# A sparse graph-attention kernel: the self edge as a copied tile, row lists over all columns, two gathered extra tiles instead of three

## The chip, the cores and the metric

The kernel runs on one core of a Trainium2 chip. A core has a matrix engine (TensorE; PE in the profile, its weight loads PEld), a vector engine (VectorE, DVE), an activation engine (ScalarE, ACT), GpSimd (POOL), a sync engine that issues transfers (SyncE, SP), and 16 DMA engines that all of its queues share. The metric is the time of the whole program on the device in microseconds; lower is better.

## What is computed

Two layers over a graph of 3327 nodes with 128 features. The adjacency matrix is dense in storage and sparse in content: about 65 of 3327 entries of a row are not zero, and the diagonal always belongs to them (the self edge).

```python
h = relu(layernorm(x))
for each of 4 heads:
    x1, x2 = h @ w1, h @ w2
    E = leaky_relu(x1[:, None, :] + x2[None, :, :], 0.01)
    s = exp(8 * tanh((E @ a) / 8)) * adj          # scores count only where adj is not zero
    out = leaky_relu((s / s.sum(-1, keepdims=True)) @ h @ Wlin.T, 0.01)
x = x + concatenate(outs) @ w
h = relu(layernorm(x))
A = adj + eye;  D = A.sum(1) ** -0.5
x = x + relu((D[:, None] * A * D[None, :]) @ (h @ W.T + b))
```

The costly part is the first layer's score of every edge: 128 sums, a ReLU and a weighted sum for each of 4 heads. The kernel works them out for edges only.

## The kernel before

The nodes are padded to 3328 and cut into 26 row blocks of 128, and each row block into two half blocks of 64 rows (HALF). There are 52 half blocks, worked through in order. A table in HBM has a row of 709 floats (COLS) for every node: 64 columns with the adjacency weights of the current half block's rows, the node's features h, score parts, and its 512 products x2. There are two such tables, one for even and one for odd half blocks; `weights` (L573) rewrites the 64 weight columns of one while the other is in use. Row 3328 of the table is all zeros.

**The lists (`prep`, one generator for each row block).** For each of its 128 rows the kernel lists the columns that are not zero. `code` holds 3328 minus the column number, so that zero means "no edge". Line 402 multiplies (adj is not zero) with `code`, in four parts of 832 columns. Line 406 takes the eight largest codes of each of 64 segments of 52 columns (MAX8). From these, `cand` keeps, for each half of the columns, 136 candidates: four for each of 32 segments and the eight largest of the rest. Lines 435 and 437 then take the 32 largest (SLOTS) of each half of the columns, by four rounds of MAX8 and MATCH_REPLACE8 over that half's 136 candidates: 64 slots for a row. Lines 458 and 461 take up to 40 more (EXTRA) by rounds over both halves together, 272 candidates. The slots become the row numbers of the gathers: `idx` (L451). The extras of all rows of a half block are packed one behind another into three tiles of 128 places (OVT): `lower` and a matrix product (L479) give each row its first place, `oi` (L496, L498) is the 0/1 matrix of 128 rows by 768 places that says which row owns which place, and `idxo` (L521) holds the table rows for these places. If a list or the tiles don't suffice, `flag` is raised, and the program ends with a dense computation of both layers, which this data doesn't need.

**The gathers (`gather`).** A half block has four windows of 8 tiles `g`, each of 128 table rows, and one more window `ge` with its OVT extra tiles. Line 563 issues one indirect transfer for each tile from POOL: 4 x 8 + 3 = 35 for each half block, 1820 in all. There are four buffers for `g` windows and one for `ge`.

**The scores.** A window of 8 tiles is worked in two groups m, and the extra tiles are group 8. `stage_z` transposes the 512 products of each tile with PE into the PSUM tile `z` (L588); there are two of these. For groups 0 to 7 DVE takes the maximum with the rows' own term, which gives `r` (L600); for group 8 the own term is added by a matrix product with `oi` (L591) and ACT applies the ReLU (L597). `stage_r` (L611) sums over features with PE, `finish` makes the exponentials and the weighted sums (L619 to L659; L666 to L677 for the extra tiles), `close` the block's end and the first half of layer 2.

**The order.** The program order is written out by hand. A counter `slot` runs through the groups, six slots to a group; in each slot `advance` moves the `prep` of the next row block on by its share of 72 steps (each `yield` is one), `fetch` issues the gathers whose buffer has come free, and the small steps of `finish` and `close` get their turn. So DVE's instructions for the next block's lists stand between the `r` operations of this block, on one engine that works in order. PE also turns the next block's adjacency rows (L356); ACT copies them into `at` (L358, a ring of four buffers, `pat`) and stores them (L361).

SP issues the adjacency loads (L343), the tables' weight columns (L573), `hTb` (L425), `xn_d` (L727) and a few more. Its instructions wait in order like those of any engine.

Of the kernel before, what the change touches and what calls it, by code (L numbers as in the profile page):

```python
# [9 lines left out]
F32 = mybir.dt.float32  # L10
AF = mybir.ActivationFunctionType
OP = mybir.AluOpType
AX = mybir.AxisListType
PSUM = bass.MemoryType.PSUM

P = 128
# [45 lines left out]
HALF = 64  # L62
OVT = 3
ROW = 720
COLS = 709
# [164 lines left out]
def _sparse_layers(tc, nc, x, adj, w1, w2, a, wlin, w, gw, gb, gb_sb, gwT, x_sb, dinv, flag, ident, out):  # L230
# [24 lines left out]
    with ExitStack() as l0:  # L255
# [25 lines left out]
        pb = l0.enter_context(tc.tile_pool(name="pb", bufs=2))  # L281
        pat = l0.enter_context(tc.tile_pool(name="pat", bufs=4))
        ph = l0.enter_context(tc.tile_pool(name="ph", bufs=2))
# [18 lines left out]
        nc.vector.tensor_scalar(hoff[:, :1], rowid, float(HALF), float(OVT * P), op0=OP.is_ge, op1=OP.mult)  # L302
        nc.vector.tensor_scalar(hoff[:, 1:], hoff[:, :1], float(OVT * P), None, op0=OP.add)
        nc.vector.tensor_scalar(rowid, hoff[:, :1], -HALF / (OVT * P), rowid, op0=OP.mult, op1=OP.add)
# [40 lines left out]
        def prep(b, k):  # L345

            adjb = blks[b].adjb
            csum = pb.tile([P, 4], F32, name="csum")
            deg = pb.tile([P, 1], F32, name="deg")
# [47 lines left out]
            for sgm in range(64):  # L397
                if sgm % 32 == 0:
                    codes = pa.tile([P, 2, part], mybir.dt.uint16, name="codes")
                    for i in range(2):  # L400
                        c0 = (sgm // 16 + i) * part
                        nc.vector.scalar_tensor_tensor(codes[:, i], adjb[:, c0:c0 + part], 0.0, code[:, c0:c0 + part],  # L402
                                                       op0=OP.not_equal, op1=OP.mult, accum_out=csum[:, sgm // 16 + i:sgm // 16 + i + 1])
                        yield
                c = sgm // 32
# [25 lines left out]
            k.lists = lists  # L431
            for c in range(2):
                for r in range(SLOTS // 8):
                    top = lists[:, SLOTS * c + 8 * r:SLOTS * c + 8 * r + 8]
                    nc.vector.max(top, cand[:, c, :SOME])
                    yield
                    nc.vector.match_replace(out=cand[:, c, :SOME], in_to_replace=top, in_values=cand[:, c, :SOME], imm_value=0.0)
                    yield

# [14 lines left out]
            yield  # L454
            flat = cand[:, :, :SOME]
            for r in range(EXTRA // 8):
                top = lists[:, 64 + 8 * r:64 + 8 * r + 8]
                nc.vector.max(top, flat)
                yield
                if r < EXTRA // 8 - 1:  # L460
                    nc.vector.match_replace(out=flat, in_to_replace=top, in_values=flat, imm_value=0.0)
                yield

# [24 lines left out]
            miss = pb.tile([P, 1], F32, name="miss")  # L488
            nc.vector.tensor_reduce(miss, csum, AX.X, OP.add)
            nc.vector.tensor_tensor(miss, lsum, miss, OP.not_equal)  # L490
# [4 lines left out]
            oi = pb.tile([P, 2 * OVT * P], F32, name="oi")  # L495
            nc.vector.tensor_scalar(oi, code[:, :2 * OVT * P], ext[:, 40:41], None, op0=OP.is_le)  # L496
            yield
            nc.vector.scalar_tensor_tensor(oi, code[:, :2 * OVT * P], end, oi, op0=OP.is_gt, op1=OP.mult)  # L498
            k.oi = oi
# [52 lines left out]
        def gather(b, hb, w):  # L552
# [3 lines left out]
            if w == NW:  # L556
                g, n, at = pe_.tile([P, OVT, WIDE], F32, name="ge"), OVT, k.idxo[:, hb]
            else:
                g, n, at = rows_in(), WT, k.idx[:, w, WT * hb:WT * hb + WT]
# [748 lines left out]
```

## Time and profile before

| | us |
|---|---|
| median of 3 runs | 3226.23 (3220.43 to 3227.33) |
| profiled execution, first to last instruction (span) | 2534.6 |
| median less that span | 691.6 |
| PE busy | 2282.7 (90%) |
| DVE busy | 2030.0 (80%) |
| POOL busy | 1792.0 (71%) |
| ACT busy | 705.3 (28%) |
| 16 DMA engines, share of the span by queue | POOL 71.1%, SP 19.1%, ACT 6.9% |
| moved | 838.58 MB |

The span is counted from the first to the last instruction that the profiler shows; the time of a run is that of the whole program, and the profiled execution has no separate one. A line of the profile's groups gives line, engine, operation, the tile that is written and those read, the count, then the busy time in us, the mean in ns of one, and how long the engine was idle just before, with what ended most of that idle time. A line of a timeline gives start and duration in us. Names are those of the code, without buffer numbers: `g`, `ge`, `z`, `r`, `lists`, `cand`, `oi`.

### The profile page before, as it was taken

Reading aid. Unit: us, or ns where it says so; the run is one execution under the profiler, and the core shown is the slowest. Engines: PE = TensorE matmul, PEld = TensorE weight load, DVE = VectorE, ACT = ScalarE, POOL = GpSimd, SP = SyncE. Lnnn points to the kernel's source line nnn. Section 1 sums busy time; section 2 is a strip of 40 time slices with the busy share of each in tenths; the row PEclk is TensorE's granted clock in tenths of the full one; section 3 lists DMA queues with packets and bytes.
Section 4 is the critical chain, followed back from the end, with each engine's and each line's share of the span. In section 5 each row is a group of like instructions: output and inputs, shape, how many; then the busy total and the mean of one; then the engine's idle time right before and its main releaser. Section 6 shows DMA issues by size and latency. Waiting matters only on the chain.

```text
span 2534.6 us, 51985 instructions
## 1 busy us (share of the span) xinstructions
PE 2282.7 (90%) x19410; PEld 1590.3 (63%) x19410; DVE 2030.0 (80%) x6260; ACT 705.3 (28%) x1651; POOL 1792.0 (71%) x1873
## 2 busy tenths in 40 slices
PE   6689999989988998999999999999999899999898
PEld 3466666666666666666666666666666666675553
DVE  7588988788887888888889888987988888795443
ACT  4122233223223222322322332232232223222110
POOL 3577777777777777777777777777777777777620
PEclk9699999999999999999999999999999999999999
DMA  9999999999999999999999999999999999999995
GB/s 298 389 333 334 332 357 317 329 352 334 315 338 343 319 327 358 324 328 344 339 316 340 355 314 338 348 334 321 343 344 317 324 361 314 332 323 343 328 333 196
DMA packets 460758, 838.58 MB, mean 331 GB/s; under 512 B 209098, under 2 KB 318164, under 8 KB 457172
## 3 DMA queue, kind: packets, MB, share of 16 engines
q0 software_dynamic: 145600, 640.34, 71.1%
q1 hardware_dynamic: 219396, 140.96, 19.1%
q10 hardware_dynamic: 95504, 53.88, 6.9%
q8 instruction: 156, 2.56, 0.4%
q14 instruction: 102, 0.84, 0.1%
HBM read 765.93 MB, written 113.42 MB: 347 GB/s over the span
## 4 chain that ended last, share of the span: by engine, by line
PE 36%; DVE 22%; DMA 20%; POOL 12%; issue 8%; ACT 0%; SPq 0%; DVEq 0%; POOLq 0%; ACTq 0%
DMA g<-table,idx 12%; POOL g L563 11%; DVE r L600 10%; PE z L588 10%; PE s L611 6%; DMA ge<-table,idxo 3%; PE z L591 3%; DMA AT_d<-at 2%; PE z L938 2%; DVE cand L406 2%; PE tr L628 2%; PE ag L659 2%; PE tr L371 1%; POOL ge L563 1%; DVE codes L402 1%
## 5 line engine op out<-in xcount | busy, mean ns | idle before, releaser
L563 POOL DMA_INDIRECT g<-table,idx x1664 | 1613.9, 970 | 568.4 <-issue 450.7
L588 PE MATMUL z<-ident,g 128*128 128x128 f32 x6656 | 929.9, 279 | 143.5 <-DVE r L600 106.2
L600 DVE TENSOR_TENSOR r<-z,x1n 128x1024 f32<-128x1024 f32 x832 | 1009.4, 1215 | 55.8 <-PE z L588 54.0
L588 PEld LDWEIGHTS z<-ident,g 128*128 128x128 f32 x6656 | 748.7, 142 | 361.7 <-DVE r L600 219.6
L611 PE MATMUL s<-r,sel 128*32 128x512 f32 (+1 forms) x3744 | 491.8, 598 | 0.7 <-ACT ssb L619 0.7
L619 ACT COPY ssb<-s 128x512 f32<-128x512 f32 x260 | 147.0, 565 | 533.9 <-PE s L611 531.4
L631 DVE TENSOR_TENSOR sc<-tr,g 128x32 f32<-128x32 f32 x208 | 38.4, 185 | 303.4 <-PE tr L628 303.4
L406 DVE MAX8 cand<-codes 128x8 f32<-128x52 uint16 x1664 | 214.9, 203 | 0.0
L563 POOL DMA_INDIRECT ge<-table,idxo x156 | 155.2, 995 | 49.0 <-issue 33.5
L639 ACT ACTIVATE th<-sc 128x32 f32<-128x32 f32 x260 | 58.3, 224 | 418.4 <-DVE sc L634 417.7
L591 PE MATMUL z<-oi,x1b 128*128 128x384 f32 x416 | 172.2, 496 | 0.0
L659 PEld LDWEIGHTS ag<-g,wt 128*32 128x32 f32 x3328 | 99.4, 110 | 115.4 <-issue 101.7
L358 ACT COPY at<-tr 128x512 f32<-128x512 f32 (+1 forms) x175 | 97.2, 555 | 215.9 <-PE tr L356 206.3
L628 PE MATMUL tr<-ident,ssb 128*128 128x128 f32 x988 | 152.6, 275 | 3.0 <-ACT at L358 2.7
L611 PEld LDWEIGHTS s<-r,sel 128*32 128x32 f32 x3744 | 73.9, 108 | 110.8 <-issue 86.6
L588 PEld LDWEIGHTS z<-ident,ge 128*128 128x128 f32 x624 | 80.7, 145 | 97.0 <-issue 27.7
L597 ACT ACTIVATE r<-z 128x768 f32<-128x768 f32 x104 | 84.4, 811 | 200.4 <-PE z L591 200.4
L659 PE MATMUL ag<-g,wt 128*32 128x133 f32 x3328 | 134.0, 279 | 0.0
L588 PE MATMUL z<-ident,ge 128*128 128x128 f32 x624 | 111.5, 282 | 23.3 <-DMA ge<-table,idxo 20.0
L356 PE MATMUL tr<-ident,adjb 128*128 128x128 f32 x676 | 107.8, 282 | 22.6 <-DMA adjb<-in_adj_dram 13.5
L628 PEld LDWEIGHTS tr<-ident,ssb 128*128 128x128 f32 x988 | 114.8, 141 | 11.1 <-ACT ssb L619 7.9
L402 DVE SCALAR_TENSOR_TENSOR codes<-adjb,code 128x832 uint16<-128x832 f32 x104 | 102.2, 1019 | 12.6 <-DMA adjb<-in_adj_dram 12.6
(188 smaller groups left out, 2347.4 us busy)
## 6 DMA issues: line engine op xcount, KB each, us to landing
adjb<-in_adj_dram SPq DMA_DIRECT2D x26, 1664.0 KB, 9.8
table<-AT_d SPq DMA_DIRECT2D x52, 832.0 KB, 17.0
AT_d<-at ACTq DMA_DIRECT2D x150, 256.0 KB, 5.7
g<-table,idx POOLq DMA_INDIRECT x1664
table<-img SPq DMA_DIRECT2D x12, 1312.0 KB, 4.9
adjb<-AT_d SPq DMA_DIRECT2D x18, 512.0 KB
g<-AT_d SPq DMA_DIRECT2D x7, 1024.0 KB
g<-AT_d ACTq DMA_DIRECT2D x5, 1024.0 KB, 11.0
```

What stands on the lines that cost most here:

```text
L356: nc.tensor.transpose(pt[:, q, :], adjb[:, (j0 + q) * P:(j0 + q + 1) * P], ident)
L358: nc.scalar.copy(at[:, :n, :], pt[:, :n, :])
L402: nc.vector.scalar_tensor_tensor(codes[:, i], adjb[:, c0:c0 + part], 0.0, code[:, c0:c0 + part], op0=OP.not_equal, op1=OP.mult, accum_out= ...
L406: nc.vector.max(cand[:, c, 8:].rearrange("p (r s) -> p r s", s=32)[:, :, sgm % 32], codes.rearrange("p a b -> p (a b)")[:, sgm % 32 * SEG: ...
L563: return nc.gpsimd.indirect_dma_start(out=g[:, t, lo:COLS], out_offset=None, in_=tab, in_offset=bass.IndirectOffsetOnAxis(ap=at[:, t:t + 1 ...
L588: nc.tensor.matmul(z[:, i, q * P:(q + 1) * P], g[:, m % 2 * 4 + q, PROJ + h * D:PROJ + (h + 1) * D], ident, is_transpose=True, start=(q == ...
L591: nc.tensor.matmul(z[:, i, :n], k.x1b[:, h * D:(h + 1) * D], k.oi[:, hb * n:(hb + 1) * n], start=False, stop=True, skip_group_check=True)
L600: nc.vector.tensor_tensor(r.rearrange("p h (i s) -> p h i s", s=16), z.rearrange("p h (i s) -> p h i s", s=16), k.x1n[:, 2 * hp:2 * hp + 2 ...
L611: nc.tensor.matmul(k.s[32 * h:32 * h + 32, :n], sel[:, h, 31 - at:63 - at], rs[h // 2][:, h % 2, :n], start=(at == 0), stop=(at == 1 or m ...
L619: nc.scalar.copy(ssb[:, :nk * P], s[:, :nk * P])
L628: nc.tensor.transpose(pt[:, q, :], ssb[:, q * P:(q + 1) * P], ident)
L659: nc.tensor.matmul(ag[32 * cg:32 * cg + 32, u, :WORK], wt[:, t].rearrange("p h q -> p (h q)"), g[:, t, FEAT:FEAT + WORK], start=(w == 0 an ...
```

## The change

- The self edge is taken out of the row's codes before the lists are made: in the part of the columns that holds the block's own 128, one scalar_tensor_tensor makes the negated diagonal and its sum, and an add takes it out. In two of the 26 blocks the own columns cross from one part into the next, and both parts do this.
- The 64 slots are the 64 largest codes of the whole row: eight rounds over 272 candidates, in place of four rounds over 136 for each half of the columns. The 40 extras follow by five more such rounds, as before.
- The extra tiles of a half block are still three, but only two (FOUND) are gathered. The third holds the half block's own 64 table rows, which SP copies from the table in one plain transfer; its other 64 rows are set to zero once. `oi` keeps its shape; DVE fills the two found tiles' part, and ACT copies the identity into the third's.
- The tile `ge` is allocated once and kept; the ring `pat` has three buffers instead of four.

```diff
+FOUND = 2
-        pat = l0.enter_context(tc.tile_pool(name="pat", bufs=4))
+        pat = l0.enter_context(tc.tile_pool(name="pat", bufs=3))
 ...
-        nc.vector.tensor_scalar(hoff[:, 1:], hoff[:, :1], float(OVT * P), None, op0=OP.add)
+        nc.vector.tensor_scalar(hoff[:, 1:], hoff[:, :1], float(FOUND * P), None, op0=OP.add)
 ...
                         nc.vector.scalar_tensor_tensor(codes[:, i], adjb[:, c0:c0 + part], 0.0, code[:, c0:c0 + part],
                                                        op0=OP.not_equal, op1=OP.mult, accum_out=csum[...])
+                        lo, hi = max(c0, b * P), min(c0 + part, (b + 1) * P)
+                        if lo < hi:
+                            diag = pb.tile([P, P], F32, name="lq", bufs=1)[:, :hi - lo]
+                            mine = codes[:, i, lo - c0:hi - c0]
+                            nc.vector.scalar_tensor_tensor(diag, mine, -1.0, ident[:, lo - b * P:hi - b * P], op0=OP.mult, op1=OP.mult,
+                                                           accum_out=csum[:, sums[0]:sums[0] + 1])
+                            nc.vector.tensor_tensor(mine, mine, diag, OP.add)
+                            sums[0] += 1
 ...
-            for c in range(2):
-                for r in range(SLOTS // 8):
-                    top = lists[:, SLOTS * c + 8 * r:SLOTS * c + 8 * r + 8]
-                    nc.vector.max(top, cand[:, c, :SOME])
-                    yield
-                    nc.vector.match_replace(out=cand[:, c, :SOME], in_to_replace=top, in_values=cand[:, c, :SOME], imm_value=0.0)
-                    yield
+            flat = cand[:, :, :SOME]
+            def select(r):
+                top = lists[:, 8 * r:8 * r + 8]
+                nc.vector.max(top, flat)
+                yield
+                if 8 * r + 8 < 2 * SLOTS + EXTRA:
+                    nc.vector.match_replace(out=flat, in_to_replace=top, in_values=flat, imm_value=0.0)
+                yield
+            for r in range(SLOTS // 4):
+                yield from select(r)
 ...
+            for r in range(SLOTS // 4, SLOTS // 4 + EXTRA // 8):
+                yield from select(r)
 ...
             oi = pb.tile([P, 2 * OVT * P], F32, name="oi")
-            nc.vector.tensor_scalar(oi, code[:, :2 * OVT * P], ext[:, 40:41], None, op0=OP.is_le)
-            yield
-            nc.vector.scalar_tensor_tensor(oi, code[:, :2 * OVT * P], end, oi, op0=OP.is_gt, op1=OP.mult)
+            places = [t.rearrange("p (c e) -> p c e", c=2)[:, :, :FOUND * P] for t in (oi, code[:, :2 * OVT * P])]
+            own = oi.rearrange("p (c u e) -> p c u e", c=2, e=HALF)[:, :, 2 * FOUND:]
+            for u in range(2):
+                nc.scalar.activation(own[:, :, u], ident.rearrange("p (c e) -> p c e", c=2), AF.Copy, scale=1.0 - u)
+            nc.vector.tensor_scalar(places[0], places[1], ext[:, 40:41], None, op0=OP.is_le)
+            yield
+            nc.vector.scalar_tensor_tensor(places[0], places[1], end, places[0], op0=OP.is_gt, op1=OP.mult)
 ...
             if w == NW:
-                g, n, at = pe_.tile([P, OVT, WIDE], F32, name="ge"), OVT, k.idxo[:, hb]
+                if b + hb == 0:
+                    state["over"] = pe_.tile([P, OVT, WIDE], F32, name="ge")
+                    nc.vector.memset(state["over"][HALF:, FOUND:], 0.0)
+                g, n, at = state["over"], FOUND, k.idxo[:, hb]
+                rows = b * P + HALF * hb
+                nc.sync.dma_start(g[:HALF, FOUND, :COLS], tables[hb][rows:rows + HALF, :COLS])
```

More of the change, by code (lines that the diff above doesn't have):

```diff
@@ L347, in prep @@
             adjb = blks[b].adjb
-            csum = pb.tile([P, 4], F32, name="csum")
+            csum = pb.tile([P, 6], F32, name="csum")
+            sums = [4]
             deg = pb.tile([P, 1], F32, name="deg")
@@ L454, in prep @@
             yield
[L455 to L458, printed above, removed]
-                yield
-                if r < EXTRA // 8 - 1:
-                    nc.vector.match_replace(out=flat, in_to_replace=top, in_values=flat, imm_value=0.0)
-                yield
+            for r in range(SLOTS // 4, SLOTS // 4 + EXTRA // 8):
+                yield from select(r)
             dv = pb.tile([P, 3], F32, name="dv", bufs=4)
@@ L488, in prep @@
             miss = pb.tile([P, 1], F32, name="miss")
-            nc.vector.tensor_reduce(miss, csum, AX.X, OP.add)
+            nc.vector.tensor_reduce(miss, csum[:, :sums[0]], AX.X, OP.add)
             nc.vector.tensor_tensor(miss, lsum, miss, OP.not_equal)
```

## The prediction

> **What bounds the kernel now.** I read the page's head first, then the wait list, then the timelines of one row block.
>
> ```profile
> span 2534.6 us, 51985 instructions
> PE 2282.7 (90%) x19410; PEld 1590.3 (63%) x19410; DVE 2030.0 (80%) x6260; ACT 705.3 (28%) x1651; POOL 1792.0 (71%) x1873
> ...
> L563 POOL DMA_INDIRECT g<-table,idx x1664 | 1613.9, 970 | 568.4 <-issue 450.7
> ...
> L563 POOL DMA_INDIRECT ge<-table,idxo x156 | 155.2, 995 | 49.0 <-issue 33.5
> ```
> POOL looks 71% busy, but nearly all its idle time is "issue": 0.30 us ahead of every gather, released by nothing. Its timeline:
>
> ```profile
> 1249.86 0.94 POOL L563 DMA_INDIRECT ge<-table,idxo  x1 [0.30 <-DMA AT_d<-at]
> 1251.11 0.95 POOL L563 DMA_INDIRECT ge<-table,idxo  x1 [0.30 <-issue]
> 1252.36 0.95 POOL L563 DMA_INDIRECT ge<-table,idxo  x1 [0.30 <-issue]
> 1253.61 1.19 POOL L563 DMA_INDIRECT g<-table,idx  x1 [0.30 <-issue]
> ```
> One gather starts every 1.25 us from 103 to 2381 us, with hardly a pause: 35 x 1.25 plus the longer ones is a half block's 44.9 us. POOL sets the pace. How much would PE and DVE win if it were faster? The wait list says (PE and PEld see the same stalls twice):
>
> ```profile
> DVE sc L631 <- PE tr L628: 306.2, 105, 7.6
> ...
> PEld z L588 <- DMA g<-table,idx: 33.6, 50, 2.1
> ...
> PEld z L588 <- DMA ge<-table,idxo: 24.9, 26, 2.3
> ...
> PE z L588 <- DMA g<-table,idx: 21.8, 33, 1.8
> ...
> PE z L588 <- DMA ge<-table,idxo: 20.0, 24, 2.0
> ```
> Only 25 to 58 us of 2534.6: PE meets the gathers about once in a block, at the extra tiles of its second half. So a second bound lies close behind POOL. The end of one block's DVE work shows it, DVE first, then PE:
>
> ```profile
> 1259.57 0.29 DVE L435 MAX8 lists<-cand 128x8 f32<-128x136 f32 x1
> ...
> 1260.17 1.21 DVE L600 TENSOR_TENSOR r<-z,x1n 128x1024 f32<-128x1024 f32 x1
> ...
> 1263.63 0.28 DVE L437 MATCH_REPLACE8 cand<-lists,cand 128x136 f32<-128x136 f32 x1
> 1270.23 0.19 DVE L631 TENSOR_TENSOR sc<-tr,g 128x32 f32<-128x32 f32 x1 [6.32 <-PE tr L628]
> ```
> ```profile
> 1259.70 0.33 PE L588 MATMUL z<-ident,ge 128*128 128x128 f32 x1
> 1260.98 0.33 PE L588 MATMUL z<-ident,ge 128*128 128x128 f32 x1 [0.94 <-DMA ge<-table,idxo]
> 1262.14 0.33 PE L588 MATMUL z<-ident,ge 128*128 128x128 f32 x1 [0.84 <-DMA ge<-table,idxo]
> ```
> From 1222.8 to 1263.9 DVE never stops: codes, MAX8 and list rounds lie between its r operations, and PE's next z waits for r ("z L588 <- DVE r L600" 107.2 us). PE begins the extra tiles at 1259.70, right behind the r that ends at 1259.65, waits 1.8 us for the gathers, and then works 8 us alone while DVE idles 6.3. A block is two such DVE stretches (about 40 and 38 us) and two PE stretches.
>
> **Gathers.** 52 of 1820 go. POOL's path gets 52 x (0.995 + 0.30) = 67 us shorter, 2.6 us per block. That is time only as far as PE waited for gathers. I take the stall at the extra tiles, 25 us (24 steady blocks x 1.04), since it lies where DVE is idle anyway; the g stalls lie in the start-up block (seven of them, 6.7 us, in PE's timeline from 76 to 122 us) and inside continuous DVE work, and I take none of them. Ends: 20 us (the PE row of ge alone) and 58 us (both PEld rows). Term: -25.
>
> **List rounds.** Eight rounds of MAX8 and MATCH_REPLACE8 now run over 272 candidates instead of 136. The rows for both sizes:
>
> ```profile
> L435 DVE MAX8 lists<-cand 128x8 f32<-128x136 f32 x208 | 61.4, 295 | 1.3
> L437 DVE MATCH_REPLACE8 cand<-lists,cand 128x136 f32<-128x136 f32 x208 | 59.0, 284 | 0.0
> L458 DVE MAX8 lists<-cand 128x8 f32<-128x272 f32 x130 | 57.3, 441 | 2.7
> ...
> L461 DVE MATCH_REPLACE8 cand<-lists,cand 128x272 f32<-128x272 f32 x104 | 44.3, 426 | 0.0
> ```
> (441-295) + (426-284) = 288 ns a round, 2.30 us a block, 60 us in all. The counts and the places in DVE's order stay. In the block above four rounds and the fifth's MAX8 stand ahead of the r (1260.17) after which PE owns the time: 4 x 0.288 + 0.146 = 1.30 us, in a stretch without DVE idle time. The rest falls into the 6.3 us idle behind it. 24 x 1.30 = +31. Ends: 0 (all absorbed) and 24 x 2.30 = 55.
>
> **Self edges.** Each block gets one scalar_tensor_tensor over 128 with an accumulator (nearest: L725, the same form, 0.279 + a read of 0.08) and one add (nearest: L377, 0.273), each waiting for the one before: 0.60 us, twice in the two blocks whose own columns cross a part's border. They stand inside the 40 us DVE stretch, so on the path: 24 x 0.60 = +14 (ends 0 and 17).
>
> **The selection matrix oi.** 512 columns instead of 768 on DVE: a third of 0.53 and of 0.94 (L496 and L498, from start to next start) is 0.18 + 0.31, of which start-up doesn't shrink; I take 0.42, in DVE's other stretch, where PE waits for L498 by name. 24 x 0.42 = -10 (ends 0 and -12). The two ACT copies cost about 0.2 each (nearest: L474, 0.194) on an engine that is 28% busy: 0, and if their cover went, +10.
>
> **Own rows.** One SP transfer of 64 rows per half block, about 0.47 us to issue (the table store L573 took that). It waits for PE's L677 and DVE's am of the half block before; there L677 ended at 1239.6. Behind it on SP stand hTb (went at 1237.5, would slip 2 us, and is first read by L527, some 65 us later), the adjb load (1250.7), the weights' store (1262.4) and xn_d: none is reached sooner than 1239.6 but hTb. So 0; a table store that slipped by those 2 us would add 2 us to 52 half blocks at most, 104, but its 17 us to landing end long before POOL needs it. PE transposes as many tiles as before; its third z of the extra tiles now waits for this transfer, sent some 10 us ahead of the two gathers. The memset of the unused half runs once, beside a DVE wait of 1.99 us at 34 us: 0.
>
> **Ring of "at".** A block's seven copies stand 3.2 us apart (1226.5 to 1246.0), so with three buffers one comes free after 9.7 us against a landing of 6.7 median, 14.0 at most. A few ACT waits of up to 4 us, behind ACT's idle time: 0, with +10 as the far end.
>
> **First block.** Its DVE work is 2.9 us later, but the first gather (66.5) came 6.8 us after its indices (59.7), and PE then waits for gathers (79.9) and adjb (86.1): 0. The last block has no list work behind it and layer 1 is untouched: 0.
>
> **Sum.** -25 + 31 + 14 - 10 = +10 us on the span of 2534.6. The profiled execution has no time of its own beside its span; the runs' median, 3226.23, stands 691.6 above it, which I carry over. 3226.2 + 10 = 3236, 0.3% slower.
>
> A rule from the Trainium skill speaks against the transfer's move: "DMA: Bandwidth & Descriptors", section "Issuing engines are not separate DMA queues", says that DMAs from all engines run on the same 16 DMA engines, so that another issuer saves only issue time. The trace agrees that these are nearly full (busy share 0.99 from 300 to 2300 us), yet POOL's even step shows that issue time is what counts. If the shared engines were the bound, only the bytes of 64 rows would be saved: a gather took 71.1% x 2534.6 / 1820 = 0.99 us of them, half of it by 52 is 26 us, not 67. The sum above stays below either.
>
> **Rivals.** A, faster: the DVE stretch has slack and POOL's relief comes through. For it: POOL's unbroken step. Against it: 41 us with no DVE gap. Price: all PE-row stalls go (20 + 21.8 = 42), oi gives 10, the self edges cost 14: 3188. It decides where DVE's added time ahead of the last r stays below 25/24 = 1.04 us a block. B, no change: gain and additions cancel, 3226; for this the terms need be off by only 4 us. C, slower still: a new wait takes the old one's place, as the 6.3 us of DVE idle shrink and all eight rounds reach the path: 24 x (2.30 + 0.60) - 25 - 10 + 10 for the ring = +45, 3271. D, the change doesn't hold on this data and the dense fallback runs, at a price that no row here shows: counted from the inputs, the fullest half block needs 240 of its 256 extra places, so 1 in 100.
>
> **How the numbers follow.** Chances: forecast 0.42, A 0.23, B 0.21, C 0.13, D 0.01. What separates from no change here is 0.2%, 6.4 us. Slower 0.42 + 0.13 + 0.01 = 0.56, same 0.21, faster 0.23. The range: down to 3203, which leaves about half of A below; up to 3262, half of C above. The forecast's own is 3233 to 3250. All lower ends together (-58 + 0 + 0 - 12 = -70) would give 3156, all upper ones (-20 + 55 + 17 + 0 + 20 = +72) 3298; that they fall together is in what is left out.
>
> **What would show it.** In the profile after: POOL's gathers stop at PE's L659 and its steps are no longer even (if they are even and the span is 40 us or more shorter, A). "z <- DMA ge" is gone from PE's waits. MAX8 and MATCH_REPLACE8 in the list lines take 441 and 426 throughout; DVE busy is near 2030 + 60 + 16 - 12 = 2094. The wait "z <- DVE r" is longer than 107. I am wrong if DVE shows gaps between the list rounds, or SP's own-rows transfer holds a table store.

## The result: 3% slower, outside the range, and a second level of times

| | us | ratio to before (95%) |
|---|---|---|
| before, median of 4 | 3223.33 (3216.62 to 3227.33) | |
| changed, median of 4 | 3321.82 (3316.31 to 3326.16) | 1.0297 [1.0265, 1.0329] |

The forecast was 3236, with a range of 3203 to 3262: the sign was right, the size was not, and 3322 lies above the range. (One run of e12 below, 4481, and one of e16, 3894, stand far above the others of their kernels, and no figure here includes them.)

The page of the changed kernel, its head, its chain and the two list rows:

```profile
span 3314.4 us, 52238 instructions
PE 2614.3 (79%) x19410; PEld 1787.3 (54%) x19410; DVE 2116.4 (64%) x6345; ACT 702.4 (21%) x1703; POOL 1734.2 (52%) x1821
...
PEclk8789988899999888998999899888899899999999
...
PE 50%; DVE 17%; another core or an unknown queue 16%; ACT 6%; issue 5%; DMA 3%; POOL 1%; ACTq 0%; SPq 0%; DVEq 0%; POOLq 0%
...
L446 DVE MAX8 lists<-cand 128x8 f32<-128x272 f32 x338 | 148.3, 439 | 4.1
...
L449 DVE MATCH_REPLACE8 cand<-lists,cand 128x272 f32<-128x272 f32 x312 | 132.8, 426 | 0.0
```

And its waits (who waited for what, us in total, times, longest):

```profile
POOL g L581 <- PE ag L677: 741.5, 172, 11.0
DVE sc L649 <- PE tr L646: 418.3, 112, 8.4
...
DVE r L618 <- remote: 227.8, 87, 12.2
...
PE z L606 <- DVE r L618: 222.5, 129, 7.5
...
ACT ssb L637 <- remote: 202.3, 27, 15.2
...
PE z L606 <- DMA g<-table,idx: 4.5, 6, 1.5
```

The shown profile of before has a span of 2534.6 us, and nothing in the change can add 780 us. This run of the changed kernel took 3316.31, so only 1.9 us lie outside its span of 3314.4; nothing like the 691.6 us that I carried over is there. POOL, which hardly paused in the shown profile of before, now waits 741.5 us for PE to free its buffers. And a releaser appears that the shown profile of before does not have: "remote", or in the chain "another core or an unknown queue", which stands here, on one core, for a wait whose end the trace can't put down to an instruction that had just finished.

**Two levels.** The runs that follow were made in groups; each group ran on one chip, with runs of the kernel before among them. All runs of a group share one of two levels: before took 2532, 2532 and 2533 in three groups and 3301, 3300 and 3224 in three others, beside the 3223 of the table above. One chip had both, in different groups. The timed runs of before and of the change stand at the upper level; the profile that I read stands at the lower one. No run of before at 3223 has a profile; e7, at 3280, stands in for them below. So there are two questions: what the change does at each level, and why.

### The profile page after: what moved, and what is told of

It reads as the page before. It is cut to its first block, busy times and chain, and to the rows that moved or that the text cites. A ratio compares the mean times of both kernels' runs of the same rounds, so it can differ in the third digit from the quotient of the medians.

```text
span 3314.4 us, 52238 instructions
## 1 busy us (share of the span) xinstructions
PE 2614.3 (79%) x19410; PEld 1787.3 (54%) x19410; DVE 2116.4 (64%) x6345; ACT 702.4 (21%) x1703; POOL 1734.2 (52%) x1821
## 4 chain that ended last, share of the span: by engine, by line
PE 50%; DVE 17%; another core or an unknown queue 16%; ACT 6%; issue 5%; DMA 3%; POOL 1%; ACTq 0%; SPq 0%; DVEq 0%; POOLq 0%
PE z L606 17%; PE s L629 10%; DVE r L618 8%; PE z L609 4%; PE tr L646 4%; ACT r L615 2%; PE tr L373 2%; PE tr L358 2%; PE ag L677 2%; DVE cand L416 2%; ACT ssb L637 2%; PE z L956 2%; ACT adjb L437 1%; DMA g<-table,idx 1%
## 5 line engine op out<-in xcount | busy, mean ns | idle before, releaser
L581 POOL DMA_INDIRECT g<-table,idx x1664 | 1612.1, 969 | 1337.9 <-PE ag L677 741.5
L606 PE MATMUL z<-ident,g 128*128 128x128 f32 x6656 | 1051.4, 303 | 324.7 <-DVE r L618 222.5
L606 PEld LDWEIGHTS z<-ident,g 128*128 128x128 f32 x6656 | 857.2, 157 | 566.0 <-DVE r L618 331.6
L629 PE MATMUL s<-r,sel 128*32 128x512 f32 (+1 forms) x3744 | 569.1, 619 | 24.0 <-issue 18.8
L646 PE MATMUL tr<-ident,ssb 128*128 128x128 f32 x988 | 176.8, 305 | 121.8 <-ACT ssb L637 87.0
L677 PE MATMUL ag<-g,wt 128*32 128x133 f32 x3328 | 194.1, 282 | 77.6 <-issue 76.0
L677 PEld LDWEIGHTS ag<-g,wt 128*32 128x32 f32 x3328 | 119.6, 111 | 223.2 <-issue 205.2
L581 POOL DMA_INDIRECT ge<-table,idxo x104 | 98.7, 949 | 107.2 <-PE ag L695 52.0
L373 PE MATMUL tr<-at,x_sb 128*128 128x128 f32 x488 | 82.9, 316 | 89.9 <-ACT at L360 61.2
L446 DVE MAX8 lists<-cand 128x8 f32<-128x272 f32 x338 | 148.3, 439 | 4.1
L449 DVE MATCH_REPLACE8 cand<-lists,cand 128x272 f32<-128x272 f32 x312 | 132.8, 426 | 0.0
```

The source lines that it names most:

```text
L373: nc.tensor.matmul(pq[:, :P], x_sb[:, j0 + q, :], at[:, q, :], start=(q == 0), stop=(q == js[-1]))
L581: return nc.gpsimd.indirect_dma_start(out=g[:, t, lo:COLS], out_offset=None, in_=tab, in_offset=bass.IndirectOffsetOnAxis(ap=at[:, t:t + 1 ...
L606: nc.tensor.matmul(z[:, i, q * P:(q + 1) * P], g[:, m % 2 * 4 + q, PROJ + h * D:PROJ + (h + 1) * D], ident, is_transpose=True, start=(q == ...
L629: nc.tensor.matmul(k.s[32 * h:32 * h + 32, :n], sel[:, h, 31 - at:63 - at], rs[h // 2][:, h % 2, :n], start=(at == 0), stop=(at == 1 or m ...
L646: nc.tensor.transpose(pt[:, q, :], ssb[:, q * P:(q + 1) * P], ident)
L677: nc.tensor.matmul(ag[32 * cg:32 * cg + 32, u, :WORK], wt[:, t].rearrange("p h q -> p (h q)"), g[:, t, FEAT:FEAT + WORK], start=(w == 0 an ...
```

## Experiments

### The kernel before, profiled again (e0, e7)

No edit.

> The kernel before, unchanged, profiled again. What is asked: the shown profile of before had a span of 2534.6 us where its runs took 3226; the profile after has a span of 3314.4 for a run of 3316.3, 2 us outside it. Theory 1 (the shown profile of before was no picture of its timed runs: in those, PE, DVE and ACT pace it, not POOL): span about 3221, 2 us below the time; a half block about 57 us instead of 44.9; POOL's gathers wait for PE's L659 in hundreds of us as they do after. Theory 2 (the 691.6 us are a fixed part outside the span, and the change itself cost them): span again near 2535, POOL's gathers 1.25 us apart.

> The kernel before, unchanged, once more with a profile beside these runs. At the lower level: span near 2531, POOL's gathers 1.25 us apart. At the upper level: span near 3221, and its waits show what holds the kernel there before any change: by theory 1, ACT and DVE waiting for landings of transfers, and POOL waiting for PE.

At the lower level (e0) a run of 2532.97 us, at the upper (e7) one of 3279.99. The page of e0 and some of its waits, then the page of e7:

```profile
span 2531.0 us, 51985 instructions
...
PE 34%; DVE 26%; DMA 19%; POOL 12%; issue 8%; ACT 0%; SPq 0%; DVEq 0%; POOLq 0%; ACTq 0%
```
```profile
PE z L588 <- DVE r L600: 110.8, 152, 2.0
...
PE z L588 <- DMA ge<-table,idxo: 22.5, 25, 2.3
...
POOL g L563 <- PE ag L659: 7.2, 4, 2.2
```
```profile
span 3278.1 us, 51985 instructions
PE 2595.6 (79%) x19410; PEld 1764.9 (54%) x19410; DVE 2049.7 (63%) x6260; ACT 688.1 (21%) x1651; POOL 1798.1 (55%) x1873
...
PE 44%; DVE 19%; another core or an unknown queue 16%; issue 7%; DMA 6%; ACT 5%; POOL 2%; SPq 0%; ACTq 0%; DVEq 0%; POOLq 0%
```

The waits of e7:

```profile
POOL g L563 <- PE ag L659: 579.7, 178, 10.3
DVE sc L631 <- PE tr L628: 455.5, 107, 8.8
...
DVE r L600 <- remote: 276.4, 100, 5.7
...
PE z L588 <- DVE r L600: 170.2, 161, 6.8
```

Theory 1 of the expectations holds: in both, 1.9 us or so lie outside the span, and at the upper level the kernel before already shows POOL waiting for PE and the "remote" waits. The 691.6 us were the distance of the two levels. At the upper level POOL waits 580 us for PE before anything is changed, so less work on POOL has no wait of PE to shorten there.

What sits behind "remote" can be read from the semaphore records of the trace. PE's records give its matmuls an end that is modelled. In e0, 1 of PE's 2416 recorded semaphore updates comes over 1 us after the end of the instruction that makes it; in e7 574 of 2243 do, by up to 7.3 us, while DVE's and ACT's come within 0.02 us in both, but for a handful. So at the upper level PE's results are later than its rows say. The traces of the upper level also hold only about half as many semaphore updates as those of the lower (e7 22512, e0 43969; of DVE's, 2451 and 3873), so who ended a wait is less certain there, and part of "remote" may be records that are missing. In e7 the weight loads of L659 also come 0.68 to 0.75 us apart in over 90 places, in e0 in none. And PE's granted clock is 0.5 in 104 stretches (516 us together) against 17 (96 us). The Trainium skill, "TensorE: Matmul & The Clock Gate", Part 1, says that PE's clock is at half after an idle window of about 3.4 us and at full again after a busy one of about that length. The stretches fit the second (66 of the 104 last 3.4 us, the only shares are 0.5 and 1); whether each follows an idle window can't be read, since PE's rows end too early there. As an estimate, half speed costs at most half of the 420 us that came on top, 210 of the 747 us between the two spans: it can't be the whole difference. What makes PE late at the upper level is not shown by any run here.

### The whole change and its ring at the lower level (e8, e1, e2)

e8 has no edit against the changed kernel. e1:
```diff
-        pat = l0.enter_context(tc.tile_pool(name="pat", bufs=3))
+        pat = l0.enter_context(tc.tile_pool(name="pat", bufs=4))
```
e2 is the kernel before with the opposite edit, four to three.

> The changed kernel once more, for the level of times that it has not been seen on beside before: so far it took 1.0297 and 1.0128 of before where before takes 3223 and 3301, and its twin with four at buffers took 0.9972 where before takes 2532. Lower level, theory 1 (the ring is worth nothing, the SP transfer costs only where PE lags behind its modelled ends): ratio 0.996 to 0.999. Lower level, theory 2 (SP transfer and ring cost there too): above 1.002. Upper level: 1.012 to 1.03 by both.

> The changed kernel with the ring of at back at four buffers, all else as changed. In the profile after, ACT stood up to 8.2 us before an at copy, waiting for the landing of a store three copies earlier, and PE then waited for ACT's ssb. Ring theory: these stalls cost about 30 of the 98 us lost, so 3321 falls to about 3290 (ratio to before near 1.02), and ACT's waits before the copies shrink from some 130 us to well below 60. List theory (all 98 us are DVE's added work, and ACT's stalls only fill time that was idle): 3315 to 3325, ratio 1.028 to 1.031. Queue theory (the semaphores that SP's extra transfers shift make the waits): also unchanged, 3315 to 3325, with the waits of ACT on landings as long as before.

> The kernel before with a ring of three at buffers, nothing else changed. Ring theory: slower by about 30 us, 3255 (ratio 1.01). My forecast's zero for the ring (far end 10 us): 3223 to 3233, ratio 1.000 to 1.003. If the ring only hurts together with the longer DVE work, this run shows nothing while the changed kernel with four buffers gains.

All three fell on the lower level: the change as it is 2528.45, ratio 0.9984 [0.9966, 1.0001]; with four buffers 2524.69, 0.9972 [0.9959, 0.9986]; before with three 2533.16, 1.0006 [0.9996, 1.0016]. So at this level the change gains between nothing and 0.3%, and the ring is worth nothing that these runs can tell. The head of e8, then its waits, then its rows:

```profile
span 2528.3 us, 52238 instructions
PE 2279.8 (90%) x19410; PEld 1587.1 (63%) x19410; DVE 2096.7 (83%) x6345; ACT 711.6 (28%) x1703; POOL 1747.5 (69%) x1821
```
```profile
PE z L606 <- DVE r L618: 146.2, 198, 2.6
...
POOL g L581 <- PE ag L677: 83.9, 45, 4.2
...
PE z L606 <- DMA g<-table,idx: 4.5, 6, 1.5
```
```profile
L511 DVE SCALAR_TENSOR_TENSOR oi<-code,end,oi 128x512 f32<-128x512 uint16 x26 | 19.3, 742 | 0.0
L509 DVE TENSOR_SCALAR oi<-code,lists 128x512 f32<-128x512 uint16 x26 | 15.5, 597 | 0.0
L410 DVE SCALAR_TENSOR_TENSOR lq<-codes,ident 128x128 f32<-128x128 uint16 (+1 forms) x28 | 7.9, 283 | 1.0
L412 DVE TENSOR_TENSOR codes<-codes,lq 128x128 uint16<-128x128 uint16 (+1 forms) x28 | 7.9, 282 | 1.0
```

PE's wait for the extra tiles' gathers (22.5 us in e0) has no row any more, POOL now has slack (83.9), and PE waits longer for `r` (146.2, against 110.8 in e0).

### The parts at the lower level (e3, e10)

e3, the lists alone on the kernel before:
```diff
-            for c in range(2):
-                for r in range(SLOTS // 8):
-                    top = lists[:, SLOTS * c + 8 * r:SLOTS * c + 8 * r + 8]
-                    nc.vector.max(top, cand[:, c, :SOME])
-                    yield
-                    nc.vector.match_replace(out=cand[:, c, :SOME], in_to_replace=top, in_values=cand[:, c, :SOME], imm_value=0.0)
-                    yield
+            flat = cand[:, :, :SOME]
+            for r in range(SLOTS // 4):
+                top = lists[:, 8 * r:8 * r + 8]
+                nc.vector.max(top, flat)
+                yield
+                nc.vector.match_replace(out=flat, in_to_replace=top, in_values=flat, imm_value=0.0)
+                yield
```
e10 (and e5, below), two gathered tiles and SP's copy on the kernel before:
```diff
-                g, n, at = pe_.tile([P, OVT, WIDE], F32, name="ge"), OVT, k.idxo[:, hb]
+                if b + hb == 0:
+                    state["over"] = pe_.tile([P, OVT, WIDE], F32, name="ge")
+                    nc.vector.memset(state["over"][HALF:, OVT - 1:], 0.0)
+                g, n, at = state["over"], OVT - 1, k.idxo[:, hb]
+                rows = b * P + HALF * hb
+                nc.sync.dma_start(g[:HALF, OVT - 1, :COLS], tables[hb][rows:rows + HALF, :COLS])
```

> The kernel before with only the eight slot rounds changed to 272 candidates (rows lists of 64 over all columns; self edges stay in, three gathered extra tiles, ring of four). Added on DVE: 26 x 2.30 = 60 us. Theory 1 with DVE wholly on the path: 3223 + 60 = 3283 (ratio 1.0185). My forecast's step (1.30 of 2.30 us a block on the path): + 31 to 34, 3256 (ratio 1.010). If DVE's idle time absorbs the rounds in the state of the timed runs: 3223 to 3230 (ratio below 1.002), and the 98 us come from elsewhere.

> The kernel before with two gathered extra tiles and the third copied by SP from the own table rows, as earlier (extras in the third tile's places get no neighbours, so its output isn't the reference's). Where before takes about 3300 this took 1.0118. Lower level: POOL's path 67 us shorter and DVE's work unchanged, so by my forecast's step - 25 us (0.990); if POOL alone paces, 0.974; if DVE's stretch binds just behind, 0.996 or more. Together with the lists alone (0.9998) and the changed kernel (0.997) it says what DVE's added work takes back.

The lists alone: 2531.24, 0.9998 [0.9980, 1.0015]. Their 56 us of DVE work (2087.3 us busy against 2031.7 in e0) cost nothing as long as POOL paces. The two tiles alone: 2490.92, 0.9837 [0.9807, 0.9866], so 41 us faster. The whole change is 38 us slower than that (2528.45): what it adds on DVE, whose largest part, the rounds, costs nothing alone, takes nine tenths of the gain back once POOL is relieved. The page head of e10:

```profile
span 2489.3 us, 52101 instructions
PE 2262.7 (91%) x19410; PEld 1581.1 (64%) x19410; DVE 2030.8 (82%) x6261; ACT 704.3 (28%) x1651; POOL 1746.3 (70%) x1821
```

Where it goes can be read from the starts of PE's z transposes (L588, in e8 L606). A half block's groups begin with them; the time from the first transpose of one group to that of the next, mean of the 18 blocks 5 to 22, in us:

```
                            e0 before   e3 lists   e10 two tiles   e8 whole change
even half, group 6            6.38        6.37         6.47            6.03
odd half,  group 1            8.41        8.59         8.51            8.93
odd half,  groups 6 + 7       7.86        8.96         7.75            8.98
odd half,  extra tiles        7.02        6.38         5.50            5.56
whole block                  89.98       90.35        88.25           89.72
```

The two tiles take 1.52 us off the step of the odd half's extra tiles, where PE used to wait for them, and 1.73 off the block. The list rounds appear in groups 6 and 7: + 1.10 in e3, where the extra tiles' step gives 0.64 back because PE then comes later to gathers that are still late, and + 1.23 from e10 to e8, where nothing is left to give back. Group 1 holds the codes and the self edges: + 0.42. Group 6 of the even half holds `oi`: - 0.44. (e3's profiled run, 2540.67, was 9 us above its median; the single steps are what counts there.)

### POOL's time or the transfer's bytes (e17)

The kernel before with two gathered tiles, nothing in the third, and two small iota instructions on POOL in the third gather's place:
```diff
+            if w == NW:
+                queue.extend((k, hb, w, partial(nc.gpsimd.iota, g[:, OVT - 1, :540], [[0, 540]], base=0, channel_multiplier=0,
+                                                allow_small_or_imprecise_dtypes=True)) for t in range(2))
             queue.extend((k, hb, w, partial(one, t)) for t in range(n))
```

> The kernel before with two gathered extra tiles, nothing in the third, and in the third gather's place on POOL two small iota instructions that write zeros to the third tile (its extras get no neighbours, so its output isn't the reference's). POOL keeps an occupation of some 1.2 us and the wait for the extra tiles' buffer; the transfer's bytes go. Upper level, where two tiles without copy took 1.0108 and the own rows sent by POOL 0.9945: if POOL's earlier place for the following gathers is what costs, 0.990 to 1.002; if not, 1.008 to 1.015. Lower level, where two tiles took 0.9837: if POOL's time is the whole of that gain, back to 0.997 to 1.002; if the transfer's bytes were part of it, in between, 0.986 to 0.996.

It fell on the lower level: 2522.10, 0.9953 [0.9935, 0.9972]. With POOL occupied again, 10 us of the 41 remain, although none of the third gather's bytes move. So up to 31 us of the relief are POOL's time. Its rows on POOL:

```profile
L566 POOL DMA_INDIRECT ge<-table,idxo x104 | 103.1, 991 | 24.4 <-issue 20.0 <-DVE dv L745 1.6 <-DVE sc L640 0.5
L808 POOL IOTA ge<- 128x540 f32 x104 | 65.0, 625 | 3.9
```
The two iotas hold POOL for more than the gather did: 2 x 0.74 us from start to start, against 1.30 for a gather of `ge` in e0, so some 10 of the 31 us may be theirs (an estimate, 52 x 0.18). The steps say the same. Against e10 the odd half's extra tiles take 0.71 us more (6.21), and the even half's group 1, where PE waits for `g`, 0.66 more (5.42, where e0 had 4.98). So POOL's time is worth some 20 to 31 of the 41 us; the rest may be the bytes.

### The two tiles at the upper level (e4, e5, e13, e12)

e4 is the changed kernel; e5 is the edit of e10; e13 is e5 without the `dma_start` and with the whole third tile set to zero once; e12 is e5 with the edit of e3. e4 and e5 ran in one group (before 3301), e12 and e13 in another (before 3300).

> The changed kernel as it is, on the chip on which these runs stand beside each other. The runs of before have so far come out at two levels: 3216 to 3227 where the changed kernel was first timed, 2526 to 2543 in the runs since. Theory 1 (at the lower level nothing but the ring of three separates this kernel from the one with four buffers, which took 0.9972 of before): ratio 0.997 to 0.999, about 2527 against 2532, POOL's gathers again mostly on issue. Theory 2 (the ring or the third tile's transfer by SP is what makes the changed kernel slow wherever it runs): ratio near 1.03 here too, 2607 against 2532. If the chip is at the upper level: 1.03 again, by either theory.

> The kernel before with only two extra tiles of a half block gathered and the third copied by SP from the half block's own 64 table rows; lists, self edges and selection matrix stay. It leaves out the part of the extras whose places lie in the third tile, so its output isn't the reference's; PE, DVE and ACT execute the same instructions on other numbers. It takes 52 gathers off POOL, 67 us of POOL's path, and adds nothing on DVE. If POOL alone paces: 2532 - 67 = 2465 (ratio 0.974). By my forecast's step: - 25, 2507 (0.990). If the DVE stretch is as near a bound as POOL: - 10 or less, 2522 or more (0.996). At the upper level of times, where POOL waits for PE in hundreds of us: 0.998 to 1.002.

> The kernel before with two gathered extra tiles and nothing in the third, which stays zero (its extras get no neighbours, so its output isn't the reference's): no transfer by SP, no wait of SP. Upper level: if SP's transfer and its wait are the cause of the loss there (1.0118 with them), this falls to 0.990 to 1.000; if it is the earlier gathers of the two tiles that hit PE at a bad place, it stays at 1.008 to 1.015. Lower level: as the two tiles with the copy, 0.981 to 0.986, if the copy is free there; below 0.980 if it isn't.

> The kernel before with two gathered extra tiles, the third copied by SP, and the eight slot rounds over 272 candidates; self edges and selection matrix as before (extras in the third tile's places get no neighbours, so its output isn't the reference's). Lower level, where the two tiles alone took 2491 (0.9837) and the changed kernel 2525 to 2528: if the list rounds take back most of the gain, + 30 to 35, 2521 to 2526 (0.996 to 0.998); my forecast's terms give + 31 for the rounds and + 4 for self edges less oi. If all 60 us of the rounds reach the path: 2551 (1.007). If the self edges are the larger part: 2491 to 2505. Upper level: 1.012 to 1.02, like the two tiles alone (1.0118).

| | us | ratio |
|---|---|---|
| e4 whole change | 3341.10 | 1.0128 [1.0083, 1.0174] |
| e5 two tiles, SP's copy | 3338.76 | 1.0118 [1.0070, 1.0166] |
| e13 two tiles, no copy | 3344.61 | 1.0108 [1.0074, 1.0141] |
| e12 two tiles, SP's copy, lists | 3340.41 | 1.0121 [1.0092, 1.0150] |

At this level it is the other way round: the two gathered tiles alone lose as much as the whole change, SP's transfer and its wait are not the reason (e13), and the list rounds, self edges, `oi` and ring add nothing that these runs can tell. The + 40 us of e4 are less than half of the + 98 of the first timing, though, where before took 3223.

### Other queues for the own rows (e6, e9, e11)

e6 and e11 change one word of the changed kernel, and e9 is e6 with four `at` buffers:
```diff
-                nc.sync.dma_start(g[:HALF, FOUND, :COLS], tables[hb][rows:rows + HALF, :COLS])
+                nc.gpsimd.dma_start(g[:HALF, FOUND, :COLS], tables[hb][rows:rows + HALF, :COLS])
```
(e11 has `nc.scalar`.)

> The changed kernel with the own rows' transfer issued by POOL's queue instead of SP's; the ring stays at three. It undoes SP's new wait. My forecast priced that wait at nothing: same as the changed kernel within 0.2%, plus up to 52 x 1.25 = 65 us of POOL's path if POOL paces, of which the list rounds' cover hides most: ratio to before 0.997 to 1.010. If SP's wait holds back the table stores or adjacency loads and that costs, the time falls below the changed kernel's by more than 0.2%. At the upper level of times: near 1.03 if SP's queue is not the cause, 1.00 to 1.02 if it is.

> The changed kernel with the own rows' transfer issued by POOL and the ring of at at four. Upper level: the transfer's queue is the cause of the loss, so 0.990 to 0.998 as with the ring of three (0.9945); if the ring mattered there, below 0.990. Lower level: POOL issues 35 transfers for a half block again, so its relief is gone; if POOL's relief is what gains 0.3% there, the ratio goes up to 1.000 to 1.005 from 0.9972; if DVE and PE bound it anyway, it stays at 0.996 to 0.999.

> The changed kernel with the own rows' transfer issued by ACT's queue instead of SP's. Its wait for PE and DVE then stands in ACT's order, ahead of ssb and th. Upper level: if any queue but SP's is as good as POOL's, 0.990 to 0.998; if the hardware queues are what costs and POOL's software queue is what helps, 1.010 or more. Lower level: ACT's order is held up, by up to 10 us a half block, at a price of 0 to 1%: 0.997 to 1.007.

At the lower level the queue makes no difference: by POOL (e9) 2526.55, 0.9977 [0.9962, 0.9993], by ACT (e11) 2527.25, 0.9981 [0.9967, 0.9996]. At the upper level POOL's copy (e6) turns the loss into a gain: 3286.03, 0.9945 [0.9918, 0.9972], 55 us below e4 in the same group. I first read that as SP's fault; e13 refutes it. What e6 shares with the kernel before, and e4, e5, e12 and e13 do not, is that POOL issues 35 transfers for a half block instead of 34 (in e6 the 35th is a plain copy and no gather). The same step table for the upper level:

```
                       e7 before  e6 own by POOL  e5 two tiles  e13 no copy  e12 + lists  e4 whole
even half, group 3       8.35          8.18          10.39         10.21        10.55       10.45
whole block            119.84        120.53         122.20        122.31       122.12      121.99
```

The 2 us are lost in one place, group 3 of every even half block, in each kernel with 34 issues and in none with 35; times 26 that is 52 us. The timed run of the changed kernel has it too (9.77). (e7's run, 3279.99, is the fastest of before in its group, 21 us below the median, so its block is a little too short.) The timeline of e4 there, and below it the same step of the same kernel at the lower level (e8):

```profile
1568.47 0.45 DVE L446 MAX8 lists<-cand 128x8 f32<-128x272 f32 x1
...
1569.37 0.69 PE L646 MATMUL tr<-ident,ssb 128*128 128x128 f32 x4
1569.89 1.47 PE L606 MATMUL z<-ident,g 128*128 128x128 f32 x12
...
1571.32 0.95 POOL L581 DMA_INDIRECT ge<-table,idxo  x1 [0.30 <-PE z L606]
...
1573.45 0.19 DVE L649 TENSOR_TENSOR sc<-tr,g 128x32 f32<-128x32 f32 x1 [4.53 <-remote]
...
1575.59 1.23 DVE L618 TENSOR_TENSOR r<-z,x1n 128x1024 f32<-128x1024 f32 x1 [1.72 <-remote]
...
1576.87 0.48 PE L606 MATMUL z<-ident,g 128*128 128x128 f32 x1 [4.51 <-DVE r L618]
```
```profile
1191.44 0.60 PE L646 MATMUL tr<-ident,ssb 128*128 128x128 f32 x4
...
1191.88 1.47 PE L606 MATMUL z<-ident,g 128*128 128x128 f32 x12
...
1192.49 0.17 DVE L649 TENSOR_TENSOR sc<-tr,g 128x32 f32<-128x32 f32 x1
...
1192.80 1.22 DVE L618 TENSOR_TENSOR r<-z,x1n 128x1024 f32<-128x1024 f32 x1
...
1194.28 0.98 PE L606 MATMUL z<-ident,g 128*128 128x128 f32 x7
```

In both, the transposes `tr` end 0.6 to 0.7 us after their start by PE's row. In e8 DVE goes on 0.45 us after that; in e4 3.4 us after, and PE then waits 4.51 us for `r`. The semaphore that this `sc` waits for is PE's; its update is recorded at 1573.43, 0.02 us before `sc` starts, and DVE had been idle since 1568.92. In this step the first gather of the extra tiles starts 4.0 to 5.4 us after the step's start in e4 and e5, and from 5.6 us on in e7 and e6 (halves 20 to 32). So the shorter order of POOL puts its gathers elsewhere under PE's work, and PE is later there. That the one makes the other is argued, not shown: e17 was meant to tell it, and fell on the lower level. One half block speaks against so simple a rule: in the timed run of the changed kernel the gather of half 28 starts 6.6 us after the step's start, and the step still takes 12.2 us.

### A lighter list (e14, e15, e16)

e14 and e16 are one kernel, the change with four `at` buffers and mixed rounds; e15 has ACT's copy as well. Three rounds over each half's 136 candidates, then two over all:
```diff
-            def select(r):
+            def select(r, c=None):
                 top = lists[:, 8 * r:8 * r + 8]
-                nc.vector.max(top, flat)
+                pool = flat if c is None else cand[:, c, :SOME]
+                nc.vector.max(top, pool)
 ...
             for r in range(SLOTS // 4):
-                yield from select(r)
+                yield from select(r, r // 3 if r < 6 else None)
```

> The changed kernel with four at buffers, and its 64 slots taken by three rounds over each half's 136 candidates and two over all 272, in place of eight over 272. The fullest half block needs 241 of its 256 extra places, counted from the inputs. DVE is spared 6 x 0.288 = 1.73 us a block, 45 us. Lower level, if the list rounds are what takes the gathers' gain back: 2525 - 25 to 2525 - 34, so 2491 to 2500 (0.984 to 0.988). If something else binds: 2518 to 2525 (0.995 to 0.997). Upper level: below the changed kernel's 1.013 to 1.03 by 0 to 1%.

> The same with the own rows' transfer issued by ACT instead of SP. Lower level: as with SP within 0.3% (0.983 to 0.989), as the changed kernel was (0.9981 against 0.9984). Upper level: if a queue other than SP's is what helps, 0.985 to 0.995; if hardware queues cost there and only POOL's helps, 1.005 or more.

> The changed kernel with four at buffers and the mixed slot rounds (three over each half's 136 candidates, two over all 272) again: it took 1.0165 where before takes 3300, and hasn't been seen where before takes 2532. There, if the list rounds are what takes the gathers' 41 us back, it spares 1.73 of their 2.30 us a block: 2525 - 25 to 2525 - 34, so 2491 to 2500 (0.984 to 0.988), and it is the fastest of the correct versions. If something else binds: 2518 to 2525 (0.995 to 0.997). At the upper level again: 1.013 to 1.02.

All fell on the upper level: e14 3359.57, 1.0165 [1.0127, 1.0203]; with ACT's copy (e15) 3353.35, 1.0168 [1.0132, 1.0203]; e16, in a group whose before took 3224, 3318.58, 1.0294 [1.0243, 1.0345]. There the 45 us of DVE work that it spares gain nothing, which agrees with e12. e15 again loses with 34 issues on POOL, whatever queue copies. At the lower level, where it should gain, it was not seen. Between the two upper groups it is mostly before that differs (3224 against 3300); kernels with 34 issues take 3319 to 3360 in all of them, and this difference stays unexplained.

## Why the prediction was wrong

**The step that failed** is "691.6 above it, which I carry over". It took a profile of the lower level as a picture of runs of the upper. e7 shows 1.9 us outside the span, POOL 55% busy and 580 us of waiting for PE. POOL waits for PE in the timed run of the changed kernel too (741.5). What the sum derives from "POOL sets the pace" does not hold at that level: no gain from the gathers (e5, e13), no cost from DVE that e12 or e4 could tell. That the sign came out as forecast is luck: + 10 was to come from DVE's added work.

**What costs at the upper level** is the gathers' term itself, with the other sign (+ 38 us in e5 and + 44 in e13, against my - 25), and in the group of e4 that is all that the whole change lost (+ 40). No rival had it. C's 3271 was nearest in number but rests on the list rounds, which cost nothing there. Of the + 98 us of the first timing this explains less than half: in the two groups whose before took 3223 and 3224 the change lost 98 and its lighter form (e16) 94, and no profile shows what made before some 77 us faster there. So the failed step is shown, but the cause of the timed loss is only in part, and why PE is late stays open.

**At the lower level,** the one I had read, the same sum can be held against the parts: (26 blocks; the prediction's terms are for 24)

| term | predicted | measured, per block x 26 |
|---|---|---|
| gathers | -25 (ends -20, -58) | -40 (1.52, the extra tiles' step); -41 by e10's time |
| list rounds | +31 | +32 (1.23) |
| self edges | +14 | +11 (0.42) |
| `oi` | -10 | -11 (0.44) |
| ring, own rows, SP | 0 | 0 (e1, e2, e9, e11) |
| sum | +10 | -8; by e8's time -4 |

The row for the step of the extra tiles (20 to 25 us of waits) was too small a base: the step shrank by 1.52 us a block, not 1.04. The rest was priced well (the rounds at 1.30 us a block, measured 1.23). There the answer is rival B, no change. The sum fits only because the gathers' term gave way first: e3 shows the rounds at nothing as long as POOL paces.

**The signs I named.** POOL's gathers stop at PE's L677 (83.9 us at the lower level, 741.5 in the timed runs); "z <- DMA ge" is gone; MAX8 and MATCH_REPLACE8 take 439 and 426; at the lower level DVE is busy 2096.7 (I said 2094) and "z <- DVE r" is 146.2, in the timed run 2116.4 and 222.5. All came as said, nearly so at the upper level. They show that the change does what it says; none could tell the levels apart. Of the two signs of being wrong, DVE shows no gaps between the list rounds (4.1 us idle ahead of MAX8 in all), but SP's own-rows transfer does hold SP (e4: 46 waits for DVE's `am`, 1292.8 us in all), and e13 shows that at the upper level this costs nothing.

**Issue time or bytes.** The rule that I weighed (the Trainium skill, "DMA: Bandwidth & Descriptors", "Issuing engines are not separate DMA queues") says that another issuer saves only issue time, which is usually small beside the transfer. Here, at the lower level, issue time is the larger part: e17 puts some 20 to 31 of the 41 us down to POOL's time. Had the shared engines been the bound, the bytes alone would have given all of it, and with no bytes moved only 10 us remained.

## What to carry to other kernels

Hold the profile's span against the times before anything else: where they don't agree within a few us, the profile is of another condition, and the distance is not a constant to carry over but the first thing to explain. Price an edit against the bound that gives way: at the lower level DVE's added rounds cost nothing beside POOL's pace, and DVE's added work took 38 of 41 us back as soon as POOL was relieved. Measure parts in the condition in which they will run, since here the same part (two gathered tiles) was worth -1.6% at one level and +1.1% at the other.

## What the runs showed of the hardware

- One program and one chip gave 2532 and 3300 us in different groups of runs, before within 1.4% in each group, with PE's results up to 7.3 us later than its rows' ends in a run of the slower group (574 of 2243 updates by over 1 us) and hardly ever in the faster (1 of 2416).
- The traces of the slower groups hold about half as many semaphore updates as those of the faster (22512 to 23949 against 43254 to 44243), which tells the two conditions apart at a glance.
- At the upper level less work on DVE did not help (e14 at 1.0165 against e4 at 1.0128), and every kernel with one issue less on POOL for a half block took 1.4 to 2.2 us more in one step of the even half blocks than before did; why is not shown.
